# Edge scores of a graph layer as a maximum and a minimum instead of a sum, a ReLU and a product

## The chip, the core and the metric

The kernel runs on one core of a Trainium2 chip. The metric is the time of one execution on the device in microseconds (us). The core has a matrix engine (PE, TensorE), a vector engine (DVE, VectorE), an activation engine (ACT, ScalarE), GpSimd (POOL), and SyncE (SP), which here only issues transfers. All run beside one another, each through its own list of instructions in order, and wait for one another by semaphores. DMA engines carry the transfers that SP, ACT and POOL issue.

## The reference

Four layers run over a batch of 32 graphs of 512 nodes and 256 features; `adj` is one 512 x 512 matrix, about 98% zeros, shared by all. Layers 0 and 3 are the same function with weights of their own, and the change is in their edge scores `S`:

```python
pre_u = jnp.einsum('bud,dk->buk', h_t, W1[:d])
pre_v = jnp.einsum('bvd,dk->bvk', h_t, W1[d:])
hidden = jax.nn.relu(pre_u[:, :, None, :] + pre_v[:, None, :, :] + b1)
S = jax.nn.sigmoid(jnp.einsum('buvk,ko->buvo', hidden, W2)[..., 0] + b2[0])
a_t = jnp.einsum('buv,bud->bvd', S * A_a, h_t)
m_t = jnp.einsum('uv,bud->bvd', A_m, h_t) * h_t
z_t = beta1 * h_t + beta2 * (a_t @ Wa + ba) + beta3 * (m_t @ Wm + bm)
```

(the last line is shortened; `A_a` and `A_m` are both `adj`). Layer 1 is `z + relu((adj @ z) @ W.T + b)`. Layer 2 is an attention with a softmax over all pairs, `leaky_relu(f_i + f_j) + adj`. `S` matters only where `adj` isn't zero.

## The kernel before

The kernel counts on the chip how many entries each row of `adj` has (class `Counts`) and branches: a dense path for full matrices, and a sparse path, which is the one that runs here. In the sparse path four batches (`NB`) form a group; eight groups pass through all layers, and a group has an edge pass for layer 0 and one for layer 3, 16 in all.

**Tables.** For each node, `pre` computes both products with W1 for one batch (L570, L572), adds b1 to the u part (L574), copies the v part (L575), and SP writes both to the group's table in DRAM (`table<-puv`, L582). A table row holds four batches of 256 values, 4 KB. On the side, `pre` computes the score of each node with itself (L577, L578), since every node has a self loop.

**Edges.** `Edges` lists the nonzero entries as 36 items (`ITEMS`) of 128 edges, one edge for each partition: eight for each chunk of 128 nodes (the first eight neighbours of each node), and four panels for what is left over. `edges` runs one pass in 36 turns. For each turn a `fetch` some turns ahead (L641) makes POOL gather the rows of the v nodes (L607) into one of five buffers; the rows of the u nodes (`mine`) are loaded once a chunk by SP (L647), or gathered for panels. A turn then adds both (L686). In every other turn DVE does max(.,0) times W2 over all 1024 values (L694), and ACT sums each batch's 256 (L672); in the others DVE does it by batch in four instructions that sum as they go (L702). In the first pass of layer 0 and the last of layer 3 (those with `spare` buffers) ACT sums every turn. After every fourth turn ACT takes the exponential (L592), and DVE makes the sigmoid (L596, L597) and multiplies by the entries of `adj` (L636). Then POOL puts the scores, 16 bytes for each edge, into `cells` in DRAM by an indirect write (L601), one put a turn. `cells` is split in two halves (chunks 0 and 1, chunks 2 and 3). Two writes to one half are kept in order, so a put waits until the last one to its half has landed, and `put` takes the other half when it can (L660). The self loops' scores go to the diagonals by two SP transfers early in the pass (`own_1`, L624).

**Middle and ends.** `load` (L727) brings `cells` back as dense matrices; `middle_one` does the rest of layer 0, layers 1 and 2 and `pre` of layer 3 for a batch: sums with the scores (L840), `hT` finished by an add on DVE (L848), layer 1 (L861 on), softmax rows (L907 to L913), their transposes on PE (L952). `last` and `sums` (L1001, L1010) finish layer 3.

**Order.** The pieces of all these streams are generators, merged by times written out by hand in `sparse_path` (L1079): a group's middle stage takes one unit, with the layer 3 pass of the group before in its first half and the layer 0 pass of the next one in its second. `edge_times` spreads a pass over its window. A scheduler then sets each engine's final order, and the engines follow it strictly.

Of the kernel before, what the change touches and what calls it, by code (L numbers as in the profile page):

```python
# [16 lines left out]
P = 128  # L17
# [19 lines left out]
SPARE = NC // 2 * OWN * P + LINES  # L37
GROUP = NB * D
HELD = 8
# [8 lines left out]
class Model:  # L48


    def __init__(self, ctx, tc, a):
        nc = self.nc = tc.nc
        self.tc, self.a = tc, a
        const = self.const = ctx.enter_context(tc.tile_pool(name="const", bufs=1))
        self.ident = const.tile([P, P], F32, name="ident")
        make_identity(nc, self.ident)
        self.adj = const.tile([P, NC, N], F32, name="adj")
        for c in range(NC):
            nc.sync.dma_start(self.adj[:, c, :], a["adj"][c * P : (c + 1) * P, :])
        self.g0, self.g3 = self.gnn_first("L0_gnn"), self.gnn_first("L3_gnn")  # L60
# [36 lines left out]
    def gnn_first(self, L):  # L97
        nc, a, const = self.nc, self.a, self.const
        w = {"L": L}
        w["W1"] = self.load(f"{L}_W1", [P, 2 * DC, D], a[f"{L}_W1"].rearrange("(c p) k -> p c k", p=P))  # L100
        w["b1bc"] = self.bcast(f"{L}_b1", D)
        w["W2bc"] = const.tile([P, D], F32, name=f"{L}_W2bc")
        nc.scalar.dma_start(w["W2bc"], a[f"{L}_W2"].rearrange("k o -> (k o)").partition_broadcast(P))
        w["b2"] = self.bcast(f"{L}_b2", 1)
        w["nb2"] = const.tile([P, 1], F32, name=f"{L}_nb2")
        w["bcol"] = const.tile([P, DC, 1], F32, name=f"{L}_bcol")
        if L == "L3_gnn":
            w["bbc"] = const.tile([P, D], F32, name=f"{L}_bbc")
        for key in ("Wa", "Wm"):
            w[key] = const.tile([P, DC, D], F32, name=f"{L}_{key}")  # L110
        return w

# [63 lines left out]
class Counts:  # L176
# [3 lines left out]
    def __init__(self, ctx, m):  # L180
        nc, tc, const = m.nc, m.tc, m.const
        self.lines = const.tile([P, NC], F32, name="lines")
        self.diag = const.tile([P, NC], F32, name="diag")
        self.excess = const.tile([1, 1], I32, name="excess")
        with tc.tile_pool(name="c_sb", bufs=2) as sb, tc.tile_pool(name="c_ps", bufs=1, space=PSUM) as ps:
            ones = sb.tile([P, N], F32, name="c_ones", bufs=1)
            nc.vector.memset(ones, 1.0)
            count = sb.tile([P, NC], F32, name="count", bufs=1)
            there = sb.tile([P, NC], F32, name="c_there", bufs=1)
            for c in range(NC):  # L190
                cs, at = slice(c * P, (c + 1) * P), slice(c, c + 1)
                mask = sb.tile([P, N], F32, name="mask")
                nc.vector.scalar_tensor_tensor(
                    mask, m.adj[:, c, :], 0.0, ones, ALU.not_equal, ALU.mult, accum_out=count[:, at]
                )
                junk = sb.tile([P, P], F32, name="djunk")
                nc.vector.scalar_tensor_tensor(
                    junk, m.adj[:, c, cs], 1.0, m.ident, ALU.mult, ALU.mult, accum_out=self.diag[:, at]
                )
            nc.vector.tensor_scalar(there, self.diag, 0.0, None, ALU.not_equal)  # L200
            nc.vector.tensor_tensor(count, count, there, ALU.subtract)
            nc.vector.tensor_scalar(self.lines, count, float(-OWN), 0.0, ALU.add, ALU.max)
            pc = ps.tile([1, NC], F32, name="pc")
            nc.tensor.matmul(pc, ones[:, 0:1], self.lines, start=True, stop=True)
            half = sb.tile([1, 2], F32, name="half")
            nc.vector.tensor_reduce(half, pc.rearrange("p (h c) -> p h c", h=2), AX.X, ALU.add)
            most = sb.tile([1, 1], F32, name="most")
            nc.vector.tensor_reduce(most, half, AX.X, ALU.max)
            nc.vector.tensor_scalar(self.excess, most, float(-LINES), None, ALU.add)
# [10 lines left out]
class Edges:  # L220
# [3 lines left out]
    def __init__(self, m, pool):  # L224
# [4 lines left out]
        self.value = pool.tile([P, ITEMS], F32, name="value")  # L229
        self.inode = pool.tile([P, 2 * PANELS], I32, name="inode")  # L230

        order = [item_of(0, j) for j in range(OWN // 2)]
        for lead, other in ((0, 2), (2, 1), (1, 3)):
            for j in range(OWN // 2):
                order += [item_of(lead, OWN // 2 + j), item_of(other, j)]
# [6 lines left out]
    def value_of(self, j):  # L242
        k = self.order.index(j)
        return self.value[:, k : k + 1]

# [3 lines left out]
    def build(self, counts, adjT, lists, psum, big, tmp):  # L249
# [66 lines left out]
        for c in (0, 2, 1, 3):  # L316
# [25 lines left out]
            self.slots(js, v, there, t, row[:, at], spare)  # L342
            yield
# [55 lines left out]
class Group:  # L399

    def __init__(self, sp, w, name):
        self.w = w
        self.table = sp.dram.tile([2 * N, GROUP], F32, name=f"table_{name}")
        self.cells = sp.cells[name[0]]
        self.s = sp.grp.tile([P, ITEMS, NB], F32, name=f"s{name[0]}")
        self.self_s = sp.grp.tile([P, NC, NB], F32, name=f"self_s{name[0]}")
# [6 lines left out]
class Sparse:  # L415
# [94 lines left out]
    def setup(self):  # L510
# [6 lines left out]

        edges = self.built = self.e.build(self.counts, self.adjT, self.lists, self.psum, self.big, self.act)
# [25 lines left out]
    def setup_rest(self):  # L544
        yield from self.rest
# [14 lines left out]
    def pre(self, g, b, hT):  # L560
# [3 lines left out]
        for c in range(NC):  # L564
            cs = slice(c * P, (c + 1) * P)
            if c % 2 == 0:
# [7 lines left out]
            nc.vector.tensor_tensor(puv[:, 0, :], pp[:, 0:D], w["b1bc"], ALU.add)  # L574
            nc.scalar.copy(puv[:, 1, :], pp[:, D:])  # L575
            both = self.small.tile([P, D], F32, name="both", bufs=1)
            nc.vector.tensor_tensor(both, pp[:, D:], puv[:, 0, :], ALU.add)  # L577
            nc.vector.scalar_tensor_tensor(  # L578
                both, both, 0.0, w["W2bc"], ALU.max, ALU.mult, accum_out=g.self_s[:, c, b : b + 1]
# [31 lines left out]
    def edges(self, g, spare=()):  # L611

        nc, e, w = self.nc, self.e, g.w
        flat = "p c b -> p (c b)"
        own = g.self_s.rearrange(flat)
# [4 lines left out]
        places = g.table.rearrange("(c p k) n -> c k p n", p=P, k=2)  # L622

        def own_1():  # L624
            self.sigmoid_of(own)
            diag = self.counts.diag.unsqueeze(2).to_broadcast([P, NC, NB])
            nc.vector.tensor_tensor(g.self_s, g.self_s, diag, ALU.mult)
            for q in range(2):
                diagonal = g.cells[q][q * HALF : q * HALF + HALF * (N + 1), :]
                diagonal = diagonal.rearrange("(c p a) b -> p c a b", p=P, a=N + 1)[:, :, 0, :]  # L630
                nc.sync.dma_start(diagonal, g.self_s[:, 2 * q : 2 * q + 2, :])

        def run_1(ks):
# [3 lines left out]
            for k in range(ks.start, ks.stop):  # L637
                j = e.order[k]
                ready.append((e.half_of(j), e.cell[:, j : j + 1], g.s[:, k, :]))

        def fetch(n):  # L641
            j = e.order[n]
            c = j // OWN
            if c >= NC or c not in mine:
                t = self.gath.tile([P, GROUP], F32, name="mine", bufs=3)
                if c < NC:
                    nc.sync.dma_start(t, places[c, 0])  # L647
                    mine[c] = t
                else:
                    self.fetch(t, g, e.iu[:, j - NC * OWN : j - NC * OWN + 1])  # L650
            else:
                t = mine[c]
# [4 lines left out]
            self.fetch(rows, g, e.iv[:, j : j + 1])  # L657
            fetched[n] = rows, t
# [9 lines left out]
        def sums(k, rows):  # L668

            for b in range(NB):  # L670
                part = rows[:, b * D : (b + 1) * D]
# [3 lines left out]
        self.half = 1  # L675
        for n in range(lead):
            fetch(n)
            yield

        todo = [(2, lambda: self.exp_of(w, own)), (4, own_1)]  # L680
        done = 0
        for k in range(ITEMS):
# [3 lines left out]
            self.behind(nc.vector.tensor_tensor(rows, rows, other, ALU.add))  # L686
            if k + lead < ITEMS:
                fetch(k + lead)
            if summed:
                summed.pop(0)()  # L690
            if spare or k % 2 == 1 and k < ITEMS - 3:
                by_entry = rows.rearrange("p (b d) -> p b d", b=NB)
                w2 = w["W2bc"].unsqueeze(1).to_broadcast([P, NB, D])
                nc.vector.scalar_tensor_tensor(by_entry, by_entry, 0.0, w2, ALU.max, ALU.mult)  # L694
# [3 lines left out]
            else:  # L698
                for b in range(NB):
                    part = rows[:, b * D : (b + 1) * D]  # L700
                    at = g.s[:, k, b : b + 1]
                    nc.vector.scalar_tensor_tensor(part, part, 0.0, w["W2bc"], ALU.max, ALU.mult, accum_out=at)  # L702
            if k % 4 == 3 or k >= ITEMS - 3:
                ks = slice(done, k + 1)
                near = spare or k >= ITEMS - 5
# [350 lines left out]
def edge_times(ahead, a, b, behind, lead=LEAD):  # L1056

    step = (b - a) / ITEMS
    first = [ahead + j * min(step, (a - ahead) / lead) for j in range(lead)]
    return first + spread(even(ITEMS), a, b) + spread(even(TAIL), b, behind)  # L1060
# [18 lines left out]
def sparse_path(ctx, m, counts, xr, outr, B):  # L1079
# [7 lines left out]
        (sp.setup_rest(), spread(even(7), -0.26, -0.20), ""),  # L1087
# [275 lines left out]
```

## Time and profile before

| | us |
|---|---|
| runs | 3131.15, 3124.82, 3122.06 (median 3124.82) |
| profiled execution | 3102.14 |
| its span, first to last instruction | 3100.4 |
| mean granted PE clock | 0.941 |

The profile is of one execution. Its page gives, for groups of instructions, the busy time, the mean of one, and the idle time of the engine before them with what ended it:

```
L601 POOL DMA_INDIRECT cells<-s,cell x576 | 691.1, 1200 | 740.7 <-DMA cells<-s,cell 370.3
L607 POOL DMA_INDIRECT rows<-table,iv x554 | 663.3, 1197 | 672.7 <-DMA table<-puv 148.1
L686 DVE TENSOR_TENSOR rows<-rows,mine 128x1024 f32<-128x1024 f32 x554 | 670.8, 1219 | 164.7 <-DMA rows<-table,iv 148.8
L672 ACT ACTIVATE rows<-rows 128x256 f32<-128x256 f32 x1096 | 442.9, 407 | 516.7 <-DVE rows L694 511.1
L702 DVE SCALAR_TENSOR_TENSOR rows<-rows,L_gnn_W2bc 128x256 f32<-128x256 f32 x1120 | 415.9, 419 | 1.8
L694 DVE SCALAR_TENSOR_TENSOR rows<-rows,L_gnn_W2bc 128x1024 f32<-128x1024 f32 x274 | 332.3, 1216 | 0.3
```

Edge work (L686, L694, L702) is over half of DVE's 2302.8 busy us. The rest of DVE serves the middle stage and `pre`, in the same queue.

### The profile page before, as it was taken

To read this page: it belongs to the slowest core of one execution; us is meant where nothing else is said; L and a number is where in the kernel's file an instruction comes from. 1 tells how busy PE (TensorE), PEld (TensorE's weight loads), DVE (VectorE), ACT (ScalarE), POOL (GpSimd) and SP (SyncE) were. 2 spreads that over 40 slices of the span, in tenths; PEclk is the share of its full clock that TensorE was granted. 3 is DMA by queue.
4 is the path that set the end of the run, shared out by engine and by line. 5 is a ranking of instruction groups with operands and counts; after the bars stand their busy time and mean duration, and the time that the engine had idled before them with its cause. 6 is when DMAs were issued, how large, how long until landed. Compare 5 with 4: busy or idle time off the path is not lost.

```text
span 3100.4 us, 32465 instructions
## 1 busy us (share of the span) xinstructions
PE 2714.6 (88%) x8645; PEld 1642.5 (53%) x8646; DVE 2302.8 (74%) x6026; ACT 1337.8 (43%) x4101; POOL 1522.5 (49%) x1312
## 2 busy tenths in 40 slices
PE   6366888889998999989998999989999899889957
PEld 3133444446654565546664565545664566545636
DVE  6783886889589875989589885888679795772761
ACT  3453554445345433545354442545335343453440
POOL 1462453556346563556346562565436563450561
PEclk9688988999999999999999999999999999999978
DMA  8874556786677766786668766787568766551753
GB/s 285 282 236 152 180 174 225 237 268 213 223 224 263 235 210 219 247 282 213 227 213 258 238 197 213 242 267 237 188 216 268 251 221 208 178 174 58 234 195 115
DMA packets 302719, 679.40 MB, mean 219 GB/s; under 512 B 52672, under 2 KB 170944, under 8 KB 294336
## 3 DMA queue, kind: packets, MB, share of 16 engines
q0 software_dynamic: 120384, 406.01, 41.0%
q1 hardware_dynamic: 163184, 234.01, 22.5%
q10 hardware_dynamic: 18960, 37.24, 3.2%
q8 instruction: 70, 1.15, 0.2%
q14 instruction: 121, 0.99, 0.1%
HBM read 531.12 MB, written 146.01 MB: 218 GB/s over the span
## 4 chain that ended last, share of the span: by engine, by line
PE 51%; DVE 18%; DMA 17%; issue 6%; ACT 4%; POOL 3%; SPq 0%; POOLq 0%; ACTq 0%; DVEq 0%
PE pst L45 24%; PE pst L1001 7%; DVE rows L686 6%; DMA table<-puv 5%; DMA rows<-table,iv 5%; PE pst L570 3%; DVE rows L702 3%; PE pst L861 3%; PE pst L1010 3%; PE pst L572 3%; DMA cells<-s,cell 3%; DVE rows L694 3%; PE pst L883 2%; PE pst L840 2%; DMA SA<-cells 2%
## 5 line engine op out<-in xcount | busy, mean ns | idle before, releaser
L601 POOL DMA_INDIRECT cells<-s,cell x576 | 691.1, 1200 | 740.7 <-DMA cells<-s,cell 370.3
L607 POOL DMA_INDIRECT rows<-table,iv x554 | 663.3, 1197 | 672.7 <-DMA table<-puv 148.1
L686 DVE TENSOR_TENSOR rows<-rows,mine 128x1024 f32<-128x1024 f32 x554 | 670.8, 1219 | 164.7 <-DMA rows<-table,iv 148.8
L672 ACT ACTIVATE rows<-rows 128x256 f32<-128x256 f32 x1096 | 442.9, 407 | 516.7 <-DVE rows L694 511.1
L45 PE MATMUL pst<-adj,h 128*128 128x512 f32 x1024 | 451.3, 592 | 0.3 <-PE pst L941 0.3
L702 DVE SCALAR_TENSOR_TENSOR rows<-rows,L_gnn_W2bc 128x256 f32<-128x256 f32 x1120 | 415.9, 419 | 1.8
L45 PE MATMUL pst<-L_gnn_Wa,hT 128*128 128x256 f32 x1024 | 264.3, 410 | 118.6 <-DMA hT<-xT 64.6
L694 DVE SCALAR_TENSOR_TENSOR rows<-rows,L_gnn_W2bc 128x1024 f32<-128x1024 f32 x274 | 332.3, 1216 | 0.3
L45 PEld LDWEIGHTS pst<-adj,h 128*128 128x128 f32 x1024 | 192.8, 190 | 222.4 <-issue 218.4
L45 PEld LDWEIGHTS pst<-L_gnn_Wa,hT 128*128 128x128 f32 x1024 | 207.7, 208 | 165.8 <-issue 53.1
L45 PE MATMUL pst<-eT,feats 128*128 128x512 f32 x512 | 231.5, 606 | 12.4 <-ACT eT L953 12.4
L45 PE MATMUL pst<-adjT,zW 128*128 128x512 f32 x512 | 227.8, 597 | 6.2 <-ACT zW L865 6.2
L1001 PEld LDWEIGHTS pst<-hWa,SA 128*128 128x128 f32 x896 | 213.7, 328 | 7.7 <-issue 4.5
L1001 PE MATMUL pst<-hWa,SA 128*128 128x256 f32 x896 | 216.8, 398 | 0.0
L861 PE MATMUL pst<-WT,hT 128*128 128x256 f32 x512 | 150.3, 459 | 75.9 <-DVE hT L848 75.9
L672 ACT ACTIVATION_READ_ACCUMULATOR rows<-rows 128x1 f32 x1096 | 206.7, 189 | 0.0
L809 ACT COPY flat<-SA 128x512 f32<-128x512 f32 x128 | 137.6, 1128 | 155.0 <-PE pst L45 60.1
L840 PE MATMUL pst<-flat,hWa 128*128 128x512 f32 x448 | 196.8, 592 | 0.0
L861 PEld LDWEIGHTS pst<-WT,hT 128*128 128x128 f32 x512 | 118.0, 235 | 114.9 <-DVE hT L848 88.1
L575 ACT COPY puv<-pst 128x256 f32<-128x256 f32 x256 | 93.7, 370 | 183.8 <-DVE puv L574 168.1
L574 DVE TENSOR_TENSOR puv<-pst,bc_L_gnn_b 128x256 f32<-128x256 f32 x256 | 105.0, 416 | 90.3 <-DMA table<-puv 53.8
L45 PEld LDWEIGHTS pst<-eT,feats 128*128 128x128 f32 x512 | 97.5, 193 | 127.5 <-issue 109.8
(170 smaller groups left out, 3979.3 us busy)
## 6 DMA issues: line engine op xcount, KB each, us to landing
table<-puv SPq DMA_DIRECT2D x256, 256.0 KB, 5.5
SA<-cells POOLq DMA_DIRECT2D x64, 1024.0 KB, 7.0
h<-in_x_dram SPq DMA_DIRECT2D x64, 512.0 KB, 6.4
mine<-table SPq DMA_DIRECT2D x64, 512.0 KB, 5.3
hT<-xT SPq DMA_DIRECT2D x36, 512.0 KB, 5.1
h<-x2s SPq DMA_DIRECT2D x36, 512.0 KB, 4.1
xT<-hT ACTq DMA_DIRECT2D x32, 512.0 KB, 5.5
x2T<-yT SPq DMA_DIRECT2D x32, 512.0 KB, 5.3
```

What stands on the lines that cost most here:

```text
L45: nc.tensor.matmul(out, lhsT, rhs, start=(n == 0), stop=(n == len(pairs) - 1))
L574: nc.vector.tensor_tensor(puv[:, 0, :], pp[:, 0:D], w["b1bc"], ALU.add)
L601: self.nc.gpsimd.indirect_dma_start(out=g.cells[half], out_offset=bass.IndirectOffsetOnAxis(ap=at, axis=0), in_=s, in_offset=None)
L607: self.nc.gpsimd.indirect_dma_start(out=rows, out_offset=None, in_=g.table, in_offset=bass.IndirectOffsetOnAxis(ap=at, axis=0))
L672: self.behind(nc.scalar.activation(part, part, AF.Identity, accum_out=g.s[:, k, b : b + 1]))
L686: self.behind(nc.vector.tensor_tensor(rows, rows, other, ALU.add))
L694: nc.vector.scalar_tensor_tensor(by_entry, by_entry, 0.0, w2, ALU.max, ALU.mult)
L702: nc.vector.scalar_tensor_tensor(part, part, 0.0, w["W2bc"], ALU.max, ALU.mult, accum_out=at)
L809: self.nc.scalar.copy(flat[:, r, :], SA[r][:, :, b])
L840: nc.tensor.matmul(pz, hWa[:, r, cs], flat[:, r, :], start=(r == 0), stop=False)
L861: nc.tensor.matmul(pw[:, at], zT[:, d, cs], m.WT_1[:, d, :], start=(d + k == 0), stop=(d * k == 1))
L1001: nc.tensor.matmul(pz[:, k * D : (k + 1) * D], SA[r][:, cs, b], hWa[:, r, :], start=(r + k == 0), stop=False)
```

## The change

For a column k with weight w, w relu(u + v) equals max(w v, -w u) + w u where w is positive and min(w v, -w u) + w u where it is negative. So if W1's v columns are scaled by w and its u columns by -w, and the columns are sorted so that those of positive w come first, the score of an edge is a sum of maxima over the first columns and of minima over the rest, less one number for its u node, the sum of its u row. The boundary differs with the weights; the kernel fixes it at 144 of 256. In the 32 columns around the middle (`MIXED`) columns of negative w are flipped in sign in both parts, go through the maximum, and are multiplied by the sign after. More than 16 positive weights above or below 128 lead to the dense path.

- `sorted` sorts and scales W1 on the chip, for layer 0 ahead of the edge lists in `setup`, for layer 3 in `setup_rest`; the W2 and b1 columns come by four small POOL transfers at the start. `Counts` also counts the positive weights.
- `pre`: the add of b1 also sums the u row; one small instruction corrects the mixed columns; the self scores (L577, L578) are gone.
- A turn: maximum over 4 x 144, sign over 4 x 32, minimum over 4 x 112; then ACT sums in ordinary passes as before every other turn, in the two with `spare` in two turns of three; the other turns use one `tensor_reduce`.
- `less` subtracts the node's number ahead of the exponential. The numbers of the panels' nodes are written to DRAM by SP and gathered by POOL, four small gathers a pass.
- Self loops are four more turns (`TURNS` = 40). SP loads their v rows, and writes their scores to a diagonal each.

The core of the diff:

```diff
+TURNS = ITEMS + NC
+MIXED = slice(D // 2 - 16, D // 2 + 16)
...
+        self.cols = const.tile([P, 2, 2, DC, 1], F32, name="cols_W2_b1")
+        for k, L in enumerate(("L0_gnn", "L3_gnn")):
+            nc.gpsimd.dma_start(self.cols[:, k, 0], a[f"{L}_W2"].rearrange("(c p) o -> p c o", p=P))
+            nc.gpsimd.dma_start(self.cols[:, k, 1], a[f"{L}_b1"].rearrange("(c p o) -> p c o", p=P, o=1))
...
+    def sorted(self, w, t, psum):
...
+        nc.vector.tensor_scalar(positive, w["col"][:, 0, :], 0.0, None, ALU.is_gt)
+        pr = psum()
+        mm(nc, pr[:, 0:1], [(before, positive[:, 0:1])])
+        mm(nc, pr[:, 1:2], [(before, positive[:, 1:2]), (ones, positive[:, 0:1])])
+        mm(nc, pr[:, 2:3], [(ones, positive[:, c : c + 1]) for c in range(DC)])
...
+        for c in range(DC):
+            nc.vector.tensor_scalar(place[:, c, :], row, to[:, c : c + 1], None, ALU.is_equal)
+        for c in range(DC):
+            pt = psum()
+            for r in range(2 * DC):
+                nc.tensor.transpose(pt[:, r * P : (r + 1) * P], w["W1"][:, r, c * P : (c + 1) * P], self.ident)
+            nc.scalar.copy(W1T[:, c, :], pt)
...
+        for scale, r in ((us, 0), (vs, DC)):
+            ps = psum()
+            for k in range(2):
+                for c in range(DC):
+                    nc.tensor.matmul(
+                        ps[:, k * D : (k + 1) * D],
+                        W1T[:, c, (r + k) * P : (r + k + 1) * P],
+                        place[:, c, :],
...
+            by = scale.unsqueeze(1).to_broadcast([P, 2, D])
+            nc.vector.tensor_tensor(w["W1"][:, r : r + 2, :], by_two(ps), by, ALU.mult)
...
+        self.m.sorted(self.m.g0, self.big(F32, 2048), self.psum)
         edges = self.built = self.e.build(self.counts, self.adjT, self.lists, self.psum, self.big, self.act)
...
-            nc.vector.tensor_tensor(puv[:, 0, :], pp[:, 0:D], w["b1bc"], ALU.add)
+            nc.vector.scalar_tensor_tensor(
+                puv[:, 0, :], pp[:, 0:D], 1.0, w["bu"], ALU.mult, ALU.add, accum_out=part
+            )
             nc.scalar.copy(puv[:, 1, :], pp[:, D:])
-            both = self.small.tile([P, D], F32, name="both", bufs=1)
-            nc.vector.tensor_tensor(both, pp[:, D:], puv[:, 0, :], ALU.add)
             nc.vector.scalar_tensor_tensor(
-                both, both, 0.0, w["W2bc"], ALU.max, ALU.mult, accum_out=g.self_s[:, c, b : b + 1]
+                junk, puv[:, 0, MIXED], 1.0, w["sign"][:, 0, :], ALU.mult, ALU.mult, accum_out=mixed
             )
...
+        order = [item_of(0, j) for j in range(OWN // 2)] + [ITEMS]
         for lead, other in ((0, 2), (2, 1), (1, 3)):
             for j in range(OWN // 2):
-                order += [item_of(lead, OWN // 2 + j), item_of(other, j)]
+                two = [item_of(lead, OWN // 2 + j), item_of(other, j)]
+                order += sorted(two)
+            order.append(ITEMS + other)
...
+                self.behind(nc.vector.tensor_tensor(s, s, by, ALU.subtract))
...
+                if j < ITEMS:
+                    ready.append((e.half_of(j), e.cell[:, j : j + 1], g.s[:, k, :]))
+                else:
+                    c, half = j - ITEMS, (j - ITEMS) // 2
+                    diagonal = g.cells[half][half * HALF : half * HALF + HALF * (N + 1), :]
+                    diagonal = diagonal.rearrange("(c p a) b -> p c a b", p=P, a=N + 1)[:, c % 2, 0, :]
+                    nc.sync.dma_start(diagonal, g.s[:, k, :])
...
+            if j < ITEMS:
+                self.fetch(rows, g, e.iv[:, j : j + 1])
+            else:
+                nc.sync.dma_start(rows, places[c, 1])
...
+        nc.vector.tensor_tensor(g.less[:, 0:NC, :], g.parts[:, 0], g.parts[:, 1], ALU.add)
+        nc.sync.dma_start(g.less_dram.rearrange("(c p) b -> p c b", p=P), g.less[:, 0:NC, :])
...
-            self.behind(nc.vector.tensor_tensor(rows, rows, other, ALU.add))
+            self.behind(nc.vector.tensor_tensor(rows[:, :, first], rows[:, :, first], other[:, :, first], ALU.max))
+            nc.vector.tensor_tensor(rows[:, :, mixed], rows[:, :, mixed], sign, ALU.mult)
+            self.behind(nc.vector.tensor_tensor(rows[:, :, behind], rows[:, :, behind], other[:, :, behind], ALU.min))
...
+            if k == TURNS // 2:
+                for q in range(2 * PANELS):
+                    index = bass.IndirectOffsetOnAxis(ap=e.inode[:, q : q + 1], axis=0)
+                    nc.gpsimd.indirect_dma_start(
+                        out=g.less[:, NC + q, :], out_offset=None, in_=g.less_dram, in_offset=index
+                    )
...
-            if spare or k % 2 == 1 and k < ITEMS - 3:
-                by_entry = rows.rearrange("p (b d) -> p b d", b=NB)
-                w2 = w["W2bc"].unsqueeze(1).to_broadcast([P, NB, D])
-                nc.vector.scalar_tensor_tensor(by_entry, by_entry, 0.0, w2, ALU.max, ALU.mult)
+            if k % 3 < 2 if spare else k % 2 == 1 and k < TURNS - 3:
                 summed.append(lambda k=k, rows=rows: sums(k, rows))
...
-                for b in range(NB):
-                    part = rows[:, b * D : (b + 1) * D]
-                    at = g.s[:, k, b : b + 1]
-                    nc.vector.scalar_tensor_tensor(part, part, 0.0, w["W2bc"], ALU.max, ALU.mult, accum_out=at)
+                nc.vector.tensor_reduce(g.s[:, k, :], rows, AX.X, ALU.add)
...
+                todo.append((k + (1 if near else 2), lambda ks=ks: less(ks)))
```

## The prediction

> **What bounds the kernel now.** I read the page's busy shares first, then the table of stages, then who waited for whom on TensorE and GpSimd, then the timeline around a few of those waits.
>
> ```profile
> PE 2714.6 (88%) x8645; PEld 1642.5 (53%) x8646; DVE 2302.8 (74%) x6026; ACT 1337.8 (43%) x4101; POOL 1522.5 (49%) x1312
> ```
> ```profile
> 180.00:240.00 60.00, 31.46 (x80) 17.52 (x80) 46.63 (x78) 31.89 (x143) 41.05 (x33) 0.78 0.71 241
> ...
> 800.00:1200.00 400.00, 381.60 (x1248) 233.05 (x1247) 303.40 (x825) 169.56 (x489) 201.63 (x175) 0.98 0.72 237
> ...
> 2900.00:3000.00 100.00, 70.12 (x238) 50.19 (x238) 81.61 (x99) 56.08 (x255) 69.33 (x51) 0.89 0.67 226
> ```
>
> In a stage's row the columns are PE, PEld, DVE, ACT and POOL busy, granted clock, DMA share and GB/s. From 400 to 2900 us PE is busy 2322 of 2500 us: it is the bound there, with 178 us of gaps. The first 400 us hold 150 us of PE gaps and the last 200 us 58: there an edge pass stands alone on the path. So a saving on VectorE is worth at most those gaps. What ends them, from 400 to 2900 us (in total, times, longest), and what POOL waits for there:
>
> ```profile
> PE pst L861 <- DVE hT L848: 75.3, 20, 8.5
> PE pst L952 <- DVE ex L913: 30.6, 21, 3.3
> PE pst L952 <- DVE cols L912: 23.1, 4, 6.6
> ```
> ```profile
> POOL cells L601 <- DMA cells<-s,cell: 321.5, 141, 6.1
> POOL cells L601 <- DVE s L636: 196.7, 38, 12.7
> POOL rows L607 <- DMA table<-puv: 148.1, 8, 22.6
> ```
>
> PE waits for DVE in nearly all of them, yet the largest is not plain DVE load:
>
> ```profile
> 680.46 1.23 DVE L686 TENSOR_TENSOR rows<-rows,mine 128x1024 f32<-128x1024 f32 x1 [8.83 <-DMA rows<-table,iv]
> 681.60 0.68 DVE L848 TENSOR_TENSOR hT<-hT,pst 128x512 f32<-128x512 f32 x1
> 682.20 0.42 DVE L702 SCALAR_TENSOR_TENSOR rows<-rows,L_gnn_W2bc 128x256 f32<-128x256 f32 x1
> 682.54 0.08 DVE L702 DVE_READ_ACCUMULATOR rows<-rows,L_gnn_W2bc 128x1 f32 x1
> 682.54 0.42 DVE L702 SCALAR_TENSOR_TENSOR rows<-rows,L_gnn_W2bc 128x256 f32<-128x256 f32 x1
> ```
>
> DVE idles 8.8 us in an edge's add because its gather has not landed, and L848, which PE needs, stands behind that add. So GpSimd's queue (gathers and puts, in order) can stop DVE, and DVE PE.
>
> **The change, DVE first.** Starts in the timeline give what one instruction really takes in a row of them: 1.14 us for 1024 elements (680.46 to 681.60), 0.60 for 512, 0.35 for 256 with its accumulator read. That is 1.055 ns an element and 0.06 us fixed. An ordinary pass (14 of 16) has 36 adds (41.0 us), 16 wide max-times-W2 (18.2) and 20 x 4 narrow ones (28.0): 87.2 us. Now each of 40 turns has a max over 576 elements (0.67), a sign over 128 (0.20) and a min over 448 (0.53), together 1.40 us; 22 turns add a reduce over 1024, and some 23 small subtractions (368 in 16 passes) take 0.08 each: 56.0 + 25.1 + 1.8 = 82.9, so -4.3 a pass, -60 in 14. The two end passes go from 36 x 2.28 = 82.1 to 56.0 + 13 x 1.14 + 1.8 = 72.6: -9.5 each. In `pre`, three instructions (0.34 + 0.34 + 0.35) become 0.35 + 0.11: -0.57 x 256 = -146. DVE falls by 225 us of 2303.
>
> No wide reduce is in the trace. Its price lies between L694, one pass over as many elements (1.14), and four L702 (1.40), the same sums done piecewise; I take 1.14, being one pass. At 1.40 the saving shrinks by 334 x 0.26 = 87 us.
>
> The wide rows' means (1219 and 419 ns) overlap their successors, so I use starts. The Trainium skill (VectorE: DVE Perf Modes, "The TRN2 errata") has a fixed cost per instruction and gives an fp32 tensor_tensor (N + 151) / 0.96 ns, which speaks against cutting one add into three: as an estimate from that page a turn's three take 1.67 us and ordinary passes gain nothing, leaving only `pre`, 168 us. The same page (Rules for kernel authors) calls tensor_reduce the slowest DVE op, at one element a cycle; no run shows it yet.
>
> **ACT** sums 18 turns in place of 16 in ordinary passes, 27 in place of 36 at the ends: 14 x 8 x 0.596 - 2 x 36 x 0.596 = +24 us on an engine busy 43%, hidden under PE.
>
> **POOL** gets four more gathers of `less` per pass: 64 x (1.20 + 0.30 of issue) = 96 us. What it does with its puts is worse. In the built order, puts that follow one to the same half of the cells rise from 108 to 220 of 576, directly behind one another from 23 to 66: 36 puts are spread over more turns, fewer are ready at a time, and alternation fails. Where the second of such a pair waited, the starts lie 5.5 us apart (mean of 156 pairs). With two other operations of 1.3 us between, a pair costs 2.9 us, so 112 / 16 = 7 more pairs a pass are 20 us, with `less` 26. The cover is POOL's own waits: for DVE's s 13 us a pass (196.7 / 15), for table writes 10, for row buffers 11, and at the end 10 us between the last copy of the loaded cells (1527.4) and the matmul that takes it (1538.8). I put it at 0 in the sum. If only the waits for s are cover, 13 us a pass are left: 26 a period of two passes, 16 behind the slack, 112 in seven periods. If the gathers become smoother, it is a gain that I bound by the row wait above, 8 us a period.
>
> **SP** issues per pass four self rows (512 KB each, as L647: 5.3 us to landing), a write of `less`, and four diagonals in place of two. In order, each diagonal holds behind it table writes and hT loads until DVE's product is done, and a put to that half waits for it to land. L631 did this once per pass, with 6.1 us to landing. Four row loads are 34 MB more of 679, on DMA engines 0.7 busy; loads are asked for three turns ahead. Taken as 0 here; its cost belongs to the same bound.
>
> **Start.** Deciding the branch has some six more small DVE operations of 0.2: +1.2 us. Sorting W1 for layer 0 needs about 25 DVE operations and 25 matmuls before the first L570; much of that fits in the 11.6 us from the branch (13.4) to that matmul (25.0). But in DVE's new order layer 3's weight scaling, whose loads went out at 29.7 to 32.6, stands ahead of W1's last product. From 0 to +14; I take +7. Against it: the first put waited for a diagonal of 12.2 us (103.2 to 115.4), which now comes later: -6. The first pass -8, most of its 9.5, since DVE was busy 20 of 20 us at 100 to 120; together -6. The **end** pass has the chain on adds and products: -8.
>
> **PE's gaps in the middle.** Of 75 us behind L848 I take 30: in one of two passes its two adds now stand behind the third and within the fourth turn, ahead of the stall, and the fifth row needs no gather. Of 54 us in the softmax rows (L912, L913), where DVE was simply busy, 10.
>
> **Sum.** -6 - 8 - 30 - 10 = -54: span 3100.4 to 3046; the profiled execution 3102.1 to 3048. The runs' median, 3124.8, lies 22.7 above that execution; on its scale 3071.
>
> **Rivals.**
> 1. *POOL becomes the bound* (the other side). Same-half puts and diagonals make each pass longer than its window; rows and then the cells come late, and PE waits at the flat copy or behind edge adds. For it: the 321.5 us above, the thin slack of 10 us, and SP's queue between two puts. Against it: POOL now waits a third of a pass for others. It decides from about 8 us a pass beyond its cover. Price +112, with 40 of middle gain lost and the ends' -14 kept: 3125 + 112 - 14, some 3223 in full; half of it 3167.
> 2. *Hidden anyway*: DVE reaches the next add sooner and waits for the same gather, or, with the reduce at 1.40 (22 x 0.26 = 5.7 a pass, more than the 4.3 saved), is not relieved in ordinary passes at all; only the ends gain, 3111, and with +14 at the start 3118.
> 3. *The load matters more*: gaps for DVE (146 us in the middle) halve (-73), the start costs only its 1.2 and keeps the diagonal's 6, and both end passes gain their whole 9.5: 3125 - 73 - 24, some 3028.
>
> **How the numbers follow.** Forecast 0.48, POOL 0.32, hidden 0.12, more 0.08. A difference under 0.3% (9 us) can't be told from none. Faster: 0.46 + 0.08 + 0.05 = 0.59; same 0.07; slower 0.34, nearly all from rival 1. Time 3071. The likeliest case alone spans 3035 to 3110. The range, 3005 to 3195, takes in rival 3, the dearer reduce, and POOL up to about 5/8 of its full price.
>
> **What would show it.** Right: DVE busy near 2080, rows of max, sign and min near 0.7, 0.2 and 0.6 us, PE's waits for the hT add near 45, the stages from 800 on over 383 of 400. Rival 1: PE below 375 of 400 there, waits of puts for landings above 500 us, DVE's first maximum waiting longer for gathers than L686 did. I am wrong at the start if the first table write comes after 45 us (38.1 before), and on the reduce if it takes over 1.4 us.

## The result, and the profile after

The changed kernel takes 3225.09 us (median of 4 runs, 3222.39 to 3229.12), the one before 3125.64: a ratio of 1.0318, 95% interval 1.0299 to 1.0337. It is slower by 99 us, where 54 us less was forecast. The profiled execution took 3229.12 us with a span of 3227.3, 126.9 above the span before. Some 27 of these 126.9 lie between the two executions and not between the kernels: the traced execution of before is 23 us under its median, this one 4 us over.

The page's busy shares, and the table of stages (columns as before):

```profile
PE 2744.1 (85%) x8729; PEld 1659.1 (51%) x8730; DVE 2115.9 (66%) x5599; ACT 1346.8 (42%) x4185; POOL 1453.2 (45%) x1390
```
```profile
800.00:1200.00 400.00, 360.50 (x1170) 220.98 (x1170) 279.65 (x723) 171.41 (x528) 192.30 (x182) 0.96 0.72 231
...
2000.00:2400.00 400.00, 354.20 (x1127) 214.82 (x1126) 279.93 (x710) 167.96 (x525) 188.99 (x180) 0.94 0.72 231
```

DVE lost 187 us of work and the kernel got slower. PE's gaps over the span rose from 385.8 to 483.2 us (+97), its busy time by 29.5 at a mean granted clock of 0.934 after 0.941. Between 400 and 2800 us the gaps were 177.8 of 2400 us before and are 260.8 now; in the first 400 us they are 146 (150 before). So most of the loss is in the middle. Who waited for whom there, from 400 to 2900 us (total, times, longest), for PE and DVE:

```profile
PE pst L987 <- DVE hT L974: 145.2, 29, 16.3
PE pst L1078 <- DVE ex L1039: 43.3, 23, 5.7
PE pst L1078 <- DVE cols L1038: 12.1, 2, 7.0
```
```profile
DVE rows L809 <- DMA rows<-table,iv: 240.5, 78, 12.7
DVE puv L673 <- DMA table<-puv: 140.0, 30, 9.7
```

The same two waits of DVE in the kernel before:

```profile
DVE rows L686 <- DMA rows<-table,iv: 133.8, 44, 12.0
...
DVE puv L574 <- DMA table<-puv: 42.8, 21, 4.2
```

The add that finishes `hT` (L848 before, L974 now) keeps PE waiting 145 us in place of 75, DVE waits 240 us for gathered rows at the maximum in place of 134 at L686, and the waits for table writes grow from 43 to 140. Over the whole span, POOL's puts wait for:

```profile
POOL cells L701 <- DMA cells<-s,cell: 385.8, 167, 7.1
POOL rows L707 <- DMA less<-less: 238.6, 7, 97.3
POOL cells L701 <- DMA cells<-s: 146.3, 40, 7.3
```

Waits of puts for puts hardly moved (370.3 before). The gathers' 238.6 us behind the write of `less`, at the start of a pass, stand where 148.1 us for table writes and 96.5 for one other transfer stood before; without that write (e4) they are 257.8 us behind table writes, so they are not new. New are 146 us of puts behind the self loops' diagonals. Last, the place with the longest wait behind L974, in the timeline of all engines:

```profile
1050.55 0.58 POOL L853 DMA_DIRECT2D SA<-cells  x1 [5.05 <-DMA cells<-s,cell]
...
1051.44 1.00 POOL L701 DMA_INDIRECT cells<-s,cell  x1 [0.30 <-issue]
...
1052.43 0.57 POOL L853 DMA_DIRECT2D SA<-cells  x1
...
1061.75 1.01 POOL L701 DMA_INDIRECT cells<-s,cell  x1 [8.75 <-issue]
1063.07 0.98 POOL L707 DMA_INDIRECT rows<-table,iv  x1 [0.30 <-issue]
...
1067.82 0.76 DVE L809 TENSOR_TENSOR rows<-rows,mine 128x576 f32<-128x576 f32 x1 [10.39 <-DMA rows<-table,iv]
...
1078.92 0.68 DVE L974 TENSOR_TENSOR hT<-hT,pst 128x512 f32<-128x512 f32 x1
...
1079.74 0.77 PE L987 MATMUL pst<-WT,hT 128*128 128x256 f32 x1 [16.35 <-DVE hT L974]
```

A layer 3 pass is at its end here: its last puts go out while the finished half of `cells` is already being loaded, 1 MB at a time. In the built order the put of 1061.75 waits for the one of 1051.44, to the same half, which was issued behind the load of 1050.55. The profile names no transfer for its 8.75 us ("issue"); that it is this one is read from the built order. POOL stands for 8.75 us, the next pass's gathers stand behind it, DVE waits 10.4 us for one of them, and L974 stands behind that. The same place in the kernel before, POOL's rows alone:

```profile
1005.01 0.57 POOL L727 DMA_DIRECT2D SA<-cells  x1
...
1010.08 1.00 POOL L601 DMA_INDIRECT cells<-s,cell  x1 [3.21 <-DMA cells<-s,cell]
1011.08 0.57 POOL L727 DMA_DIRECT2D SA<-cells  x1
...
1016.35 2.15 POOL L601 DMA_INDIRECT cells<-s,cell  x1 [4.70 <-DMA cells<-s,cell]
```

There the first put starts 5 us after the load, and the second 6.3 us after the first, where it is now 10.3. That the first put now lands late because of the load just ahead of it is argued from the order, not shown. Six passes have this place. PE's waits in the 40 us from the first such load, added up from the timelines, are 85.9 us (9 to 18 each); before they were 41.8 (6 to 9), with three puts between the first and the last of the four loads in place of five. That is 44 of the 97 us by which PE's gaps grew.

### The profile page after: what moved, and what is told of

It reads as the page before. It is cut to its first block, busy times and chain, and to the rows that moved or that the text cites. A ratio compares the mean times of both kernels' runs of the same rounds, so it can differ in the third digit from the quotient of the medians.

```text
span 3227.3 us, 32823 instructions
## 1 busy us (share of the span) xinstructions
PE 2744.1 (85%) x8729; PEld 1659.1 (51%) x8730; DVE 2115.9 (66%) x5599; ACT 1346.8 (42%) x4185; POOL 1453.2 (45%) x1390
## 5 line engine op out<-in xcount | busy, mean ns | idle before, releaser
L701 POOL DMA_INDIRECT cells<-s,cell x576 | 643.1, 1117 | 872.0 <-DMA cells<-s,cell 385.8
L707 POOL DMA_INDIRECT rows<-table,iv x555 | 593.4, 1069 | 673.1 <-DMA less<-less 238.6
L793 ACT ACTIVATE rows<-rows 128x256 f32<-128x256 f32 x1156 | 467.4, 407 | 618.7 <-DVE rows L811 307.4
L809 DVE TENSOR_TENSOR rows<-rows,mine 128x576 f32<-128x576 f32 x615 | 461.3, 750 | 304.5 <-DMA rows<-table,iv 276.6
L827 DVE TENSOR_REDUCE s<-rows 128x4 f32<-128x1024 f32 x326 | 395.2, 1212 | 3.3
L811 DVE TENSOR_TENSOR rows<-rows,mine 128x448 f32<-128x448 f32 x615 | 378.9, 616 | 0.0
L987 PE MATMUL pst<-WT,hT 128*128 128x256 f32 x512 | 158.3, 474 | 150.0 <-DVE hT L974 145.2
L673 DVE SCALAR_TENSOR_TENSOR puv<-pst,L_gnn_bu 128x256 f32<-128x256 f32 x256 | 106.9, 418 | 209.5 <-DMA table<-puv 143.5
L793 ACT ACTIVATION_READ_ACCUMULATOR rows<-rows 128x1 f32 x1156 | 218.2, 189 | 0.0
L810 DVE TENSOR_TENSOR rows<-rows,L_gnn_sign 128x128 f32<-128x128 f32 x615 | 171.1, 279 | 0.0
```

Of the source, the lines that this page charges most:

```text
L701: self.nc.gpsimd.indirect_dma_start(out=g.cells[half], out_offset=bass.IndirectOffsetOnAxis(ap=at, axis=0), in_=s, in_offset=None)
L707: self.nc.gpsimd.indirect_dma_start(out=rows, out_offset=None, in_=g.table, in_offset=bass.IndirectOffsetOnAxis(ap=at, axis=0))
L793: self.behind(nc.scalar.activation(part, part, AF.Identity, accum_out=g.s[:, k, b : b + 1]))
L809: self.behind(nc.vector.tensor_tensor(rows[:, :, first], rows[:, :, first], other[:, :, first], ALU.max))
L810: nc.vector.tensor_tensor(rows[:, :, mixed], rows[:, :, mixed], sign, ALU.mult)
L811: self.behind(nc.vector.tensor_tensor(rows[:, :, behind], rows[:, :, behind], other[:, :, behind], ALU.min))
```

## The experiments

Ratios are to the kernel before on the same chip, with 95% intervals. To compare across chips, "us" is the ratio times 3125; a difference of two such figures is uncertain by some 10 to 20 us.

| kernel | ratio | us |
|---|---|---|
| changed | 1.0318 (1.0299 to 1.0337) | 3224 |
| e1 no self loops | 0.9837 (0.9783 to 0.9891) | 3074 |
| e2 diagonals from POOL | 1.0369 (1.0312 to 1.0427) | 3240 |
| e3 self rows from POOL | 1.0323 (1.0264 to 1.0383) | 3226 |
| e4 no `less` gathers | 1.0261 (1.0204 to 1.0318) | 3207 |
| e5 no diagonals | 1.0115 (1.0069 to 1.0161) | 3161 |
| e6 e1 with diagonals | 0.9963 (0.9941 to 0.9985) | 3113 |
| e7 no diagonals, no row loads | 1.0020 (0.9990 to 1.0050) | 3131 |
| e8 self turns first | 1.0262 (1.0235 to 1.0289) | 3207 |
| e9 e1 with self sums in `pre` | 1.0015 (0.9999 to 1.0031) | 3130 |
| e10 e1 with more DVE | 0.9891 (0.9861 to 0.9921) | 3091 |
| e11 e1 with more bytes | 0.9929 (0.9905 to 0.9953) | 3103 |
| e12 e1, same half preferred | 0.9787 (0.9764 to 0.9811) | 3058 |
| e13 e9 shorter, same half preferred | 0.9985 (0.9960 to 1.0011) | 3120 |
| e14 e1 with early diagonals | 0.9858 (0.9820 to 0.9896) | 3081 |
| e15 changed, same half preferred | 1.0371 (1.0326 to 1.0416) | 3241 |
| e16 before, same half preferred | 1.0047 (1.0025 to 1.0069) | 3140 |
| e17 no row loads | 1.0194 (1.0152 to 1.0237) | 3186 |
| e18 before, no self sums | 1.0022 (1.0003 to 1.0040) | 3132 |

### Is it the self loops, and is it the queue that issues them?

e1 takes the self loops out of the change:

```diff
-TURNS = ITEMS + NC
+TURNS = ITEMS
...
-        order = [item_of(0, j) for j in range(OWN // 2)] + [ITEMS]
+        order = [item_of(0, j) for j in range(OWN // 2)]
...
-            order.append(ITEMS + other)
...
-            nc.vector.tensor_copy(self.value_of(ITEMS + c), counts.diag[:, c : c + 1])
```

> The change without its self loops: 36 turns a pass, no self row loads, no diagonal writes (the diagonal of the adjacency is left out of what is computed); max and min, sorted W1 and less all stay. Theory SP (SP's ordered queue: four diagonals and four self rows a pass, whose waits hold table writes, hT loads and puts): most of the 100 us goes, 3040 to 3090. Theory POOL (puts to one half follow one another too often, and the less gathers): the turns thin the puts too, so about half goes, 3130 to 3170, the waits of puts for puts stay at about 386 us. Theory DVE (short maximum, sign and minimum in place of one add put hT behind more instructions that wait for gathers): 3190 to 3225, and the wait behind the hT add stays near 145 us.

Measured 3076.31 us (3120.21 for the kernel before on that chip). Its PE waits from 400 to 2900 us:

```profile
PE pst L1076 <- DVE ex L1037: 43.9, 9, 7.6
PE pst L985 <- DVE hT L972: 41.0, 11, 6.5
PE pst L1076 <- DVE cols L1036: 25.4, 4, 9.3
```

Self loops as items cost 150 us, half as much again as the change loses; the wait behind the `hT` add falls from 145 to 41. The theory that the short DVE operations themselves do it falls: the other turns still have them all. DVE's own waits don't tell the kernels apart: in this faster one it still waits 181 us for gathered rows at the maximum (L807) and 113 for table writes, where before it was 134 and 43.

e2 and e3 move the issue off SP:

```diff
-                    nc.sync.dma_start(diagonal, g.s[:, k, :])
+                    ready.append((half, diagonal, g.s[:, k, :]))
...
+                    nc.gpsimd.dma_start(to, s)
```
```diff
-                nc.sync.dma_start(rows, places[c, 1])
+                nc.gpsimd.dma_start(rows, places[c, 1])
```

> The four diagonals of a pass are issued by GpSimd among the puts, in alternation of halves, in place of SP. SP's queue no longer waits for them (261 us of waits at L760 in the changed kernel) but GpSimd issues 64 more. Theory SP: 3140 to 3190, the waits of puts for diagonals (146 us) shrink. Theory POOL: GpSimd gets more work, 3225 to 3260. Theory DVE: 3215 to 3230.

> The four self row loads of a pass are issued by GpSimd in place of SP; diagonals stay on SP. SP loses 438 us of waits for row buffers at L778, behind which table writes stand. Theory SP: 3150 to 3190, and VectorE's waits for table writes fall from 143 to near 60 us. Theory POOL: 3225 to 3260. Theory DVE: 3215 to 3230.

3241.68 and 3222.21 us: neither helps, where theory SP asked for 3140 to 3190. In e2 the waits only move: the diagonals, now in POOL's own queue, hold it for 85.0 us until a put to their half has landed, and puts still wait 127.1 for diagonals:

```profile
POOL cells L701 <- DMA cells<-s,cell: 446.1, 175, 7.0
...
POOL cells L701 <- DMA cells<-s: 127.1, 46, 6.4
...
POOL cells L790 <- DMA cells<-s,cell: 85.0, 41, 5.1
```

(Waits of POOL over the whole span; L790 is the diagonal in that kernel.) The Trainium skill (DMA: Bandwidth & Descriptors, "Issuing engines are not separate DMA queues") says that transfers run on the same 16 engines whoever starts them, so that another issuer saves only its own time to issue; these two runs agree, with ratios of 1.0369 and 1.0323 against 1.0318. That SP's order costs nothing is not shown by them: in e3 DVE's waits for table writes fall from 140 to 119 us, but POOL's for puts to land rise from 386 to 463, so a gain on one queue may be lost on the other.

e4 leaves out `if k == TURNS // 2:` with its four gathers, and the write that feeds them:

> The 64 gathers of less for the panels and the write that feeds them are left out (the panels' edges then subtract a wrong number); all else as in the changed kernel. Theory POOL: GpSimd has 6 us a pass less to do, 3150 to 3200. Theories SP and DVE: no change worth naming, 3205 to 3230.

3209.05 us, 18 below the changed kernel by ratio: less than the 50 that theory POOL asked for at the middle of its range, and at the edge of what these figures resolve.

### What of a self loop costs?

e5 drops the diagonal writes, e6 adds them alone to e1, e7 and e17 replace the row loads without and with diagonals:

```diff
-                    nc.sync.dma_start(diagonal, g.s[:, k, :])
+                    continue
```
```diff
+                if k in (4, 12, 20, 28):
+                    c = (0, 2, 1, 3)[k // 8]
+                    half = c // 2
...
                     nc.sync.dma_start(diagonal, g.s[:, k, :])
```
```diff
-                nc.sync.dma_start(rows, places[c, 1])
+                nc.scalar.copy(rows, self.m.adj[:, 0:2, :].rearrange("p c n -> p (c n)"))
```

> The 40 turns and the self row loads stay, the four diagonal writes of a pass are left out (the diagonal of the adjacency is missing from what is computed). In the built order puts that follow one to the same half fall from 220 to 128 of 576. Theory diagonals (each of them waits for the puts to its half, and the next put waits for it; puts come in the wrong order around them): 3070 to 3110, as without self loops (3076). Theory turns (four more turns a pass, 2.5 us of VectorE each, and 34 MB of row loads): 3190 to 3225. In between the two share it.

> 36 turns and no self rows, but four diagonal writes a pass at the places of the changed kernel (of other edges' values: the diagonal computed is another). In the built order 202 of 576 puts follow one to the same half. Theory diagonals: 3150 to 3215. Theory turns: 3075 to 3100.

> As the kernel without diagonals, and the four self row loads of a pass are replaced by a copy on ScalarE from a tile that stands in SBUF (1.1 us each; the sums of the self turns are of other numbers). Theory diagonals: no change against it. Theory turns, by the bytes and by SP's waits for row buffers: 40 to 100 us below it; by VectorE's 2.5 us a turn: equal to it.

> The changed kernel with its diagonals, but the four self row loads of a pass replaced by a copy on ScalarE from a tile in SBUF (the self sums are of other numbers). It fills the square of diagonals and row loads at 40 turns: both 3225, rows alone 3151, neither 3122. If the row loads and the diagonals hurt each other on SP's ordered queue: 3140 to 3165, the diagonal costing about 31 as it did at 36 turns. If the diagonals and the turns hurt each other, whatever is loaded: 3185 to 3205.

3151.02, 3107.30, 3121.99 and 3188.45 us. Both theories were too simple: e5 and e6 lie between their two ranges. The steps, by ratio:

| | no diagonal | diagonals late |
|---|---|---|
| 36 turns | 3074 (e1) | 3113 (e6) |
| 40 turns, no row loads | 3131 (e7) | 3186 (e17) |
| 40 turns, row loads | 3161 (e5) | 3224 |

Late diagonals cost 39 alone, 55 and 63 among 40 turns; the row loads 30 and 38; four more turns 57. So the 150 us are some 57 + 30 + 39 and 24 that appear only together, near what can't be told from chance. Among kernels with 40 turns PE's wait behind the `hT` add follows: 145.2, then in e5 and e7 from 400 to 2900 us

```profile
PE pst L987 <- DVE hT L974: 81.0, 26, 8.8
```
```profile
PE pst L987 <- DVE hT L974: 62.9, 21, 8.7
```

e10 and e11 put one suspected cost each into e1, with `idle` a tile of its own:

```diff
+            if k in (4, 12, 20, 28):
+                self.behind(nc.vector.tensor_tensor(idle[:, :, first], seen[:, :, first], seen[:, :, first], ALU.max))
...
+                nc.vector.tensor_reduce(self.m.idle_s, idle, AX.X, ALU.add)
```
```diff
+            if k in (4, 12, 20, 28):
+                nc.sync.dma_start(self.m.idle, places[(0, 2, 1, 3)[k // 8], 1])
```

> The kernel without self loops, with a maximum, a sign, a minimum and a reduce on a tile of its own added in four turns of each pass (2.5 us of VectorE each, 160 us in all; nothing waits for them and they wait for no transfer). If VectorE's time is what a self turn costs: 3105 to 3125. If not: 3076 to 3090.

> The kernel without self loops, with four loads of 512 KB a pass by SP into a tile that nobody reads (34 MB in all; each waits only for the load before it). If a self row's bytes are what it costs: 3095 to 3120. If its wait for a row buffer does, or the turn: 3074 to 3088.

3093.75 and 3102.96 us; e10 lies between its two ranges. 34 MB that nobody reads or waits for cost 29 us, give or take 18, as much as the row loads did (30): the bytes are enough to explain those, without a wait for a buffer. 144 us more of DVE busy time (1985.0 to 2129.3) cost 17, which alone can't be told from none. So DVE's time explains some 17 of the 57 us of four more turns a pass; the other 40 stay open (slots, buffers held, or the 60 us of copies that e7 itself adds on ACT). With 36 turns the wait behind the `hT` add doesn't follow the time: in e11, 29 us above e1, it is 3.8 us, and PE waits for `mhT` instead, 54 us.

### Can the diagonals be put early?

e8 keeps everything and puts the self turns first (`SELVES`), with two early diagonal writes; e14 is e1 with two early writes:

```diff
+        order = [ITEMS + c for c in SELVES] + [item_of(1, j) for j in range(OWN // 2)]
+        for lead, other in ((1, 3), (3, 0), (0, 2)):
...
+                    nc.sync.dma_start(diagonal, g.s[:, ks, :])
```

> All of the change is kept, but the four self turns stand first in a pass, and two diagonal writes (one for each half) follow them before any put of the pass has to be made; for it the chunks' tiles of two self turns are loaded a second time (17 MB in all). Theory diagonals: 3080 to 3130, waits of puts for diagonals under 30 us. Theory turns: 3200 to 3260, since the turns are all there and more is loaded.

> The kernel without self loops, plus two diagonal writes a pass early, as in the kernel before, of numbers that stand there anyway; no self sums in pre. It splits the 53 us between the kernel without self loops (3076) and the one with self sums in pre (3129). If early diagonals cost nothing and VectorE's work inside pre does: 3070 to 3090. If any diagonal write among puts costs: 3100 to 3130.

3198.11 and 3085.48 us. Early writes cost about 7 where there are no self turns, which can't be told from none, and in e8 no put waits for a diagonal any more; but e8 is only 17 below the changed kernel. The forecast for it was wrong, as it laid the whole cost to the diagonals: the turns and loads are still there, and 17 MB more. Where e8 loses the rest wasn't followed up.

### Puts to the same half

The rival of the prediction priced these. e12, e16 and e15 prefer the same half in e1, in the kernel before and in the changed one:

```diff
-            at = next((n for n, r in enumerate(ready) if r[0] != self.half), 0)
+            at = next((n for n, r in enumerate(ready) if r[0] == self.half), 0)
```

> The kernel without self loops, in which a put to the same half as the one before is preferred, not avoided: 190 of 576 puts follow one to their half in the built order, in place of 108 (220 in the changed kernel). If same-half puts cost what the prediction's rival said (2.9 us a pair, beyond the cover): 3100 to 3150. If GpSimd's waits cover them: 3072 to 3095.

> The kernel before with the put to the same half preferred: 184 same-half puts in place of 108. By the prediction's price of 2.9 us a pair it would be 150 to 220 us slower where nothing covers it. If GpSimd's waits cover it: 3100 to 3130.

> The changed kernel with the put to the same half preferred. The built order has as many same-half puts as before it (224 for 220), so: 3210 to 3235 if only the order that was built counts.

3055.43, 3141.45 and 3241.37 us: 16 below, 15 above and 17 above their partners by ratio. All three lie outside the ranges written for them. With 184 same-half puts in place of 108 the kernel before moves by 0.5%, far less than the price asked for. The signs differ, and e15 has practically the same count of such puts as the changed kernel. So an order built differently moves this kernel by some 15 us either way, and nothing smaller is explained below. Nor is it their number that makes late diagonals dear: e6 has 202 such puts and is 39 above e1, e12 has 190 and is 16 below it.

### Where is the gain without self loops from?

e9 keeps the new edge and sums the self loops in `pre`; e18 takes the self sums out of the kernel before; e13 is e9 with one operation less and the same half preferred:

```diff
+            for n, cols, op in ((0, slice(0, MIXED.start), ALU.max), (1, slice(MIXED.stop, D), ALU.min)):
...
+                nc.vector.scalar_tensor_tensor(rest, v, 1.0, puv[:, 0, cols], ALU.mult, op, accum_out=at)
...
+            nc.vector.tensor_tensor(junk, v, puv[:, 0, MIXED], ALU.max)
...
```
```diff
-            nc.vector.tensor_tensor(both, pp[:, D:], puv[:, 0, :], ALU.add)
-            nc.vector.scalar_tensor_tensor(
-                both, both, 0.0, w["W2bc"], ALU.max, ALU.mult, accum_out=g.self_s[:, c, b : b + 1]
-            )
...
+        nc.vector.memset(g.self_s, 0.0)
```

> The change with 36 turns a pass; the self loops are not turns but four short VectorE operations for each chunk behind the bias add that writes puv (some 0.7 us, 256 times, 180 us in all, as much VectorE work as 64 self turns), and two diagonal writes a pass early, as in the kernel before. No self rows are loaded. If the cost of self loops as items is in their loads, their buffers, their slots and their late diagonals: 3080 to 3105, faster than the kernel before. If it is in VectorE's time for them: 3120 to 3160.

> The kernel before without the two VectorE operations a chunk in pre that sum the self loops (a constant is written to the diagonal, as early as before). It has the old add and W2 product for each edge, with as little in pre as the kernel with early diagonals and without self sums (3085). If all that the change gained came from pre: 3075 to 3095. If the maximum and minimum of an edge were worth 40 us themselves: 3110 to 3130.

> All that the reference asks for: the change with 36 turns, the self loops as three short operations behind the bias add (3129 with four), and the put to the same half preferred. If the gain seen without self loops (3076 to 3055) was of the put order: 3095 to 3112, faster than the kernel before. If it was chance: 3120 to 3130.

3128.70, 3136.81 and 3119.49 us. All with early diagonals: old edge with self sums in `pre` 3125, old edge without 3132, new edge with 3130, new edge without 3081 (e14). Neither saving shows by itself; the 44 us come only when both are there. PE's gaps over the span (385.8 before, 431.6 in e18, 399.8 in e9, 378.4 in e14) don't tell where: they follow the traced executions, and the one of before is 23 us under its median, that of e14 12 over. The busy shares of e9 and e14:

```profile
PE 2727.7 (87%) x8730; PEld 1645.2 (53%) x8730; DVE 2151.2 (69%) x7037; ACT 1293.5 (41%) x3913; POOL 1436.2 (46%) x1390
```
```profile
PE 2717.6 (88%) x8730; PEld 1650.7 (53%) x8730; DVE 1993.1 (64%) x5245; ACT 1293.7 (42%) x3913; POOL 1431.4 (46%) x1390
```

158 us of DVE in `pre` cost 49 (e9 less e14), where 144 us of DVE among the turns cost 17 (e10 less e1): DVE's time seems dearer in `pre`, though the two differ by little more than their uncertainty. Why the old edge gains nothing from an empty `pre` stays open: e18 lies above both ranges written for it. e13, at 0.9985, can't be told from the kernel before, so no version that computes all was found to beat it.

## Why the prediction was wrong

**What bounds the kernel** held: PE's gaps, most of them behind DVE, carry the loss. That DVE's stalls behind gathers make the gaps was seen at single places; their sum doesn't follow the time (228 us from 400 to 2900 in e6, at 3113).

**DVE's prices** held. A turn's three operations take 1.40 us from start to start, as forecast, and the reduce 1.13 (1.14 forecast), as the next rows of DVE show:

```profile
1097.62 0.75 DVE L809 TENSOR_TENSOR rows<-rows,mine 128x576 f32<-128x576 f32 x1
1098.28 0.62 DVE L811 TENSOR_TENSOR rows<-rows,mine 128x448 f32<-128x448 f32 x1
1098.82 0.28 DVE L810 TENSOR_TENSOR rows<-rows,L_gnn_sign 128x128 f32<-128x128 f32 x1
1099.02 0.69 DVE L998 TENSOR_TENSOR yT<-yT,hT 128x512 f32<-128x512 f32 x1
1099.63 1.21 DVE L827 TENSOR_REDUCE s<-rows 128x4 f32<-128x1024 f32 x1
1100.76 0.75 DVE L809 TENSOR_TENSOR rows<-rows,mine 128x576 f32<-128x576 f32 x1
```

The first column counts: 0.66, 0.54 and 0.20. The estimate of 1.67 from the Trainium skill (VectorE: DVE Perf Modes, "The TRN2 errata") is near the sum of the rows' own durations, 1.65, which overlap their successors; the starts decide. DVE fell by 187 us, where 225 were forecast; where the other 38 went wasn't followed up.

**The failed step** is the self loops as items: "Four row loads are 34 MB more of 679 [...] Taken as 0 here", and with them the diagonals on SP. They cost 150 us: some 57 for four more turns, 30 to 38 for the bytes, 39 to 63 for diagonals among the puts. That is about all of the miss, from 54 us less to 99 more; without self loops (e1) the kernel is at 3074. I had counted the turns as DVE time only, inside a saving; but a turn also takes a buffer, a slot and a load of 512 KB, and each diagonal stands in the order of the puts to its half, on either queue. What of this makes up the 57 stays open beyond some 17 for DVE. On POOL, "I put it at 0 in the sum" was near enough for what it named: the same-half puts move the kernel by some 15 us with either sign (e12, e15, e16), and the gathers of `less` cost some 18, at the edge of what can be told (e4). What it did not count there are the 146 us for which puts wait for diagonals. The prediction's 5.5 us between the starts of a pair, over 156 pairs, can't be of puts that follow one another, of which it counts 108; other puts stand between many of them.

**PE's gaps in the middle**, -30 and -10: not seen. Without self loops (e1) the gaps from 400 to 2800 us are 170.5, 7 below those of the traced execution before; as that one is 23 us under its median, a larger gain can't be ruled out. So that e1 comes near the forecast of 3071 doesn't show that the sum's other terms were right.

**The start** was late beyond the bound I set: the first table write comes at 49.9 us (38.1 before; over 45 was to be wrong). It cost nothing all the same: the first put comes at 116.5 us (116.2), and the first 400 us have 4 us fewer gaps.

**The rivals.** Rival 1 has the right time (3223 in full), which is luck, as most of its +112 was the price of same-half puts, and the right signs: stages below 375 of 400, the first maximum waiting longer for gathers than L686 did, and 532 us of waits of puts for landings, if those for diagonals count. Its place was half right: SP's diagonals between two puts are a part, 39 to 63; the same-half puts that I priced at 2.9 us a pair are not, as e12 and e16 showed. It was given 0.32, the diagonals were named in it, and the sum still took their cost as 0. Rival 2 fits e9: with the self sums back in `pre`, the cheaper edge is hidden.

## What to carry to other kernels

When a change adds items to a stream, price the whole item (its slot, buffer, bytes, and each ordered write), not only the time of the engine that it relieves: here 187 us of freed VectorE bought nothing against 64 more items. A write to a place that other writes wait for costs by where in their order it stands: two early diagonals a pass cost 7 us in all, no more than chance, four late ones 39 to 63. A cost that has a rival of its own with a chance of a third doesn't belong in the sum as 0.

## What the hardware showed unexpectedly

34 MB of loads that nobody waits for, on DMA engines about 0.7 busy, cost 29 us, give or take 18 (e11 against e1). Of two small indirect writes to one half, the first issued 0.9 us after a load of 1 MB on the same queue, the second started 10.3 us after the first (1051.44 to 1061.75). At the six places of this kind the two starts are 7.1 to 10.3 us apart, and 6.0 to 6.4 in the kernel before, where the first put came 4 to 6 us after the load; POOL stood for 5.5 to 8.75 us at each. Moving the issue of 64 transfers from SP to POOL changed nothing that can be told from chance (e2, e3).
